# Three accumulators in turn in layers 2 and 3, and the end of a layer-3 tile in four pieces

## The chip, the cores and the metric

The kernel runs on one core of a Trainium2 chip. The metric is the device time of one execution in microseconds (us). The times shown are medians of several executions, beside one execution that the hardware profiler recorded.

The engines are named as in the profile: PE (TensorE, with PEld for its weight loads), DVE (VectorE), ACT (ScalarE), POOL (GpSimd, which here issues the indirect loads), and SP (SyncE, which here issues the direct loads and stores). The engines run side by side, and each takes its own instructions in their order.

## The reference, cut to what matters

Four graph layers on 4096 nodes with 256 features; `adj` is sparse in its later rows and denser in the first. The change touches layers 2 and 3:

```
def layer2(x, adj, H_v):
    scores = x @ H_v                                  # one score a node
    logits = where(adj != 0, adj * scores[None, :], lowest)
    weights = softmax(logits, over the neighbours)
    return weights @ x

def layer3(x, adj, weight, bias):
    neighbours = adj @ x                              # 4096 x 256
    edges = einsum('ij,ji->i', adj, adj)[:, None]     # known since layer 0
    support = concatenate((x, neighbours, edges), axis=1)
    return support @ weight + bias                    # 513 x 256

x = layernorm(x + layer2(x, adj, H_v))
x = layernorm(x + layer3(x, adj, weight, bias))
```

Layers 0 and 1 (a plain adjacency product, and two steps of attention that keeps only the largest weights) come before and stay as they are.

## The kernel before

The nodes are cut into 32 tiles of 128. In layers 2 and 3 the work of a tile is a sum over neighbour columns, taken up in one PSUM accumulator on PE, and then an end that reads the accumulator.

There are two kinds of tiles. The first tiles are hubs: six in layer 2, three in layer 3 (`HUBS`, line 41). A hub goes over all 32 column tiles, in 8 chunks of 4: a panel of the transposed adjacency is loaded by SP, four buffers in turn, and each chunk gives 4 matmuls (`all_columns`, lines 1049 to 1057, in layer 2; `adj_matmul`, lines 166 to 180, in layer 3). All other tiles are listed: of each, `CAPS[I]` gathered columns of 4 to 16 entries a row are used. The packed weights (`pc`) are loaded by SP in blocks of at most 5 columns, and for each column POOL gathers 128 rows of features with an indirect DMA (`xg`, line 353) into one of 16 buffers. `listed_steps` (lines 396 to 410) then makes one matmul a column and yields after each. `listed_matmul` runs it to its end.

The order of tiles is that of `mixed(n)`: the listed tiles from the last to the first, with a hub after each run of them. In layer 2 the runs have 4 tiles, in layer 3 they have 8.

In layer 2 the weights of a column are made first: ACT takes the exp (line 1029), DVE multiplies by the mask (line 1030), into one of four `pe` buffers. The end of a tile is on DVE: `rk`, from the last column of the accumulator (lines 1072 and 1073), `y` = accumulator times `rk` plus the tile's own features (line 1061), and the layernorm. `y` is the last reader of the accumulator. The result goes to a DRAM array `x3d`, and stays in the core's memory as `X3`.

In layer 3 the end of a tile is `out_3` (lines 1077 to 1090): `nb`, a copy of the accumulator on ACT, which is its last reader; four transposes on PE into one PSUM tile, two of the tile's own features and two of `nb`; `xT`, a copy of them on ACT; four output matmuls into `po`; a bias term `t` on DVE; the sum, the layernorm, and the store by SP.

Both layers take the accumulators "R" and "A" in turn, so that tile n writes where tile n-2 has been read out. A third PSUM area, two banks under the tag "lg", serves the logits of layer 1 and lies unused in layers 2 and 3.

Apart from the attention loops of layer 1, the order in which instructions stand on their engines is not written by hand: a planner runs through the program with a model of its own, and puts on each engine, among the instructions that it holds ready, the one that comes first in program order. So the place of a line in the program is a priority, and waits on the chip can differ from those that the planner saw.

Of the kernel before, what the change touches and what calls it, by code (L numbers as in the profile page):

```python
# [11 lines left out]
F32 = mybir.dt.float32  # L12
# [6 lines left out]
P = 128  # L19
N = 4096  # L20
D = 256
# [35 lines left out]
LC = 512  # L57
# [5 lines left out]
def gnn_kernel(ctx: ExitStack, tc: tile.TileContext, x, pair, W0, W1T, W2T, W3T, U1T, U2T,  # L63
# [99 lines left out]
    adjT_v = pair.rearrange("(t p) b s i -> p t b s i", p=P)  # L163
    pair_r = pair.rearrange("j b s i -> (j b) (s i)")

    def adj_matmul(ps, rhs, I, seen=None, width=D, beside=None):

        for c in range(NT // JC):
            a = pools["loads"].tile([P, JC, P], F32, name="panel", tag="panel")
            nc.sync.dma_start(a, adjT_v[:, c * JC:(c + 1) * JC, I, 1])  # L170
            if seen is not None:
                nc.vector.tensor_reduce(seen[:, c * JC:(c + 1) * JC, I], a, AX.X, OP.max, apply_absolute_value=True)
            if beside is not None:
                beside(c)
            if callable(rhs):
                b = rhs(c)
            for k in range(JC):
                j = c * JC + k
                r = b[:, k, :] if callable(rhs) else rhs[j][:, :width]
                nc.tensor.matmul(ps[:, :width], a[:, k, :], r, start=(j == 0), stop=(j == NT - 1))  # L180

    def acc_tile(which):
        return psum.tile([P, 512], F32, name="acc", tag=f"acc{which}")
# [24 lines left out]
    def transposed(tiles, name):  # L208

        n = 2 * len(tiles)  # L210
        pt = psum.tile([P, 4, P], F32, name="ptx", tag="ms", bufs=2)
        for s, t in enumerate(tiles):
            for h in range(2):
                nc.tensor.transpose(pt[:, 2 * s + h, :], t[:, h * P:(h + 1) * P], ident)
        xT = work.tile([P, 4, P], F32, name=name, tag="xT")
        nc.scalar.copy(xT[:, :n, :], pt[:, :n, :])  # L216
        return xT
# [53 lines left out]
    def run(gen):  # L271
        for _ in gen:
            pass
# [111 lines left out]
    def unpack(I):  # L385
        parts = []
        for m, (a, b) in enumerate(pieces(I)):
            if step_one[0]:
                pc = pools["gat"].tile([P, PIECE, 2, P], F32, name="pc2", bufs=n_blocks[0])[:, :, 1]
            else:  # L390
                pc = pools["gat"].tile([P, PIECE, P], F32, name="pc", bufs=4)
            nc.sync.dma_start(pc[:, :b - a], packed[I][m])
            parts.append(pc)
        return parts

    def listed_steps(ps, src, width, I, parts, use=None, stop=True):

        n = 0
        for pc, (a, b) in zip(parts, pieces(I)):
            xs = []  # L400
            for k in range(a, b):
                xg = pools["gat"].tile([P, src.shape[1]], F32, name="xg", padded_shape=[P, D + 2])
                gather(xg, src, idx_x, col(I, k))
                xs.append(xg)
            if use is not None:
                pc = use(pc, xs, b - a)
            for k in range(b - a):
                nc.tensor.matmul(ps[:, :width], pc[:, k, :], xs[k][:, :width], start=(n == 0), stop=stop and n == CAPS[I] - 1)  # L408
                n += 1
                yield  # L410

    def listed_matmul(*args, **kw):
        run(listed_steps(*args, **kw))
# [402 lines left out]
    def times_u(pz, xT, u, start, stop):  # L816
        for h in range(2):
            nc.tensor.matmul(pz, xT[:, h, :], u[:, h, :], start=start and h == 0, stop=stop and h == 1)  # L818

    def pz_tile():  # L820
        return psum.tile([P, D], F32, name="pz", tag="ms", bufs=2)
# [218 lines left out]
    def mixed(n):  # L1040

        listed = list(range(NT - 1, n - 1, -1))
        step = -(-len(listed) // (n + 1))
        order = []
        for k in range(n + 1):
            order += listed[k * step:(k + 1) * step] + [k] * (k < n)
        return order

    def all_columns(ps, I):
        for c in range(NT // JC):  # L1050
            a = pools["loads"].tile([P, JC, P], F32, name="panel", tag="panel")
            nc.sync.dma_start(a, adjT_v[:, c * JC:(c + 1) * JC, I, 1])
            xs = X2[c * JC:(c + 1) * JC]
            e = nbr_weights(a, xs, JC)
            for k in range(JC):
                j = c * JC + k
                nc.tensor.matmul(ps[:, :D + 1], e[:, k, :], xs[k][:, :D + 1], start=(j == 0), stop=(j == NT - 1))
# [5 lines left out]
        nc.sync.dma_start(x3d[rows(I), :], x3)  # L1063

    for n, I in enumerate(mixed(HUBS[0])):
        ps = acc_tile("A" if n % 2 else "R")
        if I < HUBS[0]:
            all_columns(ps, I)
        else:
            listed_matmul(ps, x2d, D + 1, I, unpack(I), nbr_weights)  # L1070
        rk = one("rk", bufs=3)
        nc.vector.tensor_scalar_max(rk, ps[:, D:D + 1], 1e-37)
        nc.vector.reciprocal(rk, rk)
        out_2(I, ps, rk, X2[I][:, :D], X3[I])


    def out_3(I, ps, x3):
        nb = work.tile([P, D], F32, name="nb")
        nc.scalar.copy(nb, ps[:, :D])
        t = work.tile([P, D], F32, name="y")  # L1080
        nc.vector.scalar_tensor_tensor(t, web, edge[:, I:I + 1], b3b, op0=OP.mult, op1=OP.add)
        nc.vector.tensor_add(t, t, x3)
        xT = transposed([x3, nb], "xT3")
        po = pz_tile()
        for a in range(2):
            times_u(po, xT[:, 2 * a:2 * a + 2], wl[a], a == 0, a == 1)
        nc.vector.tensor_add(t, t, po)
        o = pools["late"].tile([P, D], F32, name="o", padded_shape=[P, D + 2])
        layernorm(o, t)
        nc.sync.dma_start(out[rows(I), :], o)  # L1090

    for n, I in enumerate(mixed(HUBS[1])):
        ps = acc_tile("A" if n % 2 else "R")
        if I < HUBS[1]:
            adj_matmul(ps, X3, I)
        else:
            listed_matmul(ps, x3d, D, I, unpack(I))
        out_3(I, ps, X3[I])


    def rows4(src, more=0):
# [35 lines left out]
    def with_all_columns():  # L1137
        for I in range(LE, NT):
            ps = acc_tile("A")
            adj_matmul(ps, rows4(x, 1), I, width=D + 1)  # L1140
            xin = reload(x, I)
            for _ in out_0(I, ps, ps[:, D:D + 1], xin, xin):
                pass
        feats = [pools["e"].tile([P, D], F32, name=f"all_{I}", bufs=1) for I in range(NT)]
        for I in range(NT):
            nc.sync.dma_start(feats[I], xd[0][rows(I), :])
        for n in range(2):
            U[n] = [load_u(n, s) for s in range(2)]
            if n:
                for I in range(NT):  # L1150
                    nc.sync.dma_start(feats[I], xad[rows(I), :])
            for I in range(NT):
                old = reload(xd[n], I)
                psr = acc_tile("R")
                adj_matmul(psr, rows4(xd[n]), I)
                xf = new_xf(I, psr, old)
                e, rk = attn_any(n, I)
                psa = acc_tile("A")
                weighted_sum(psa, e, feats)
                if n:  # L1160
                    run(out_1(I, xf, new_xa(xa_tile(1, I), psa, rk)))
                else:
                    xa = new_xa(work.tile([P, D], F32, name="xa3", tag="z"), psa, rk)
                    nc.sync.dma_start(xad[rows(I), :], xa)
                    run(out_a0(I, xa, feats))
                    run(out_f0(I, xf))
        sb = pools["e"].tile([P, N], F32, name="score_b", bufs=1)
        for g in range(NT // 4):
            pt = psum.tile([P, 4, P], F32, name="pt", tag="tp", bufs=2)
            for k in range(4):  # L1170
                j = g * 4 + k
                nc.tensor.transpose(pt[:, k, :], scores[:, j:j + 1].to_broadcast([P, P]), ident)
            nc.scalar.copy(sb[:, g * 512:(g + 1) * 512], pt.rearrange("p a b -> p (a b)"))
        for I in range(NT):
            nc.sync.dma_start(feats[I], x2d[rows(I), :D])
        for I in range(NT):
            e, rk = nbr_any(I, sb)
            ps = acc_tile("A" if I % 2 else "R")
            weighted_sum(ps, e, feats)
            out_2(I, ps, rk, feats[I], work.tile([P, D], F32, name="x3", tag="z"))  # L1180
        for I in range(NT):
            x3 = reload(x3d, I)
            ps = acc_tile("A" if I % 2 else "R")
            adj_matmul(ps, rows4(x3d), I)
            out_3(I, ps, x3)

    leave()
    enter(e=1, loads=2, tmp=1)
# [32 lines left out]
```

## Time and profile before

| | us |
|---|---|
| median of 3 runs | 3561.51 (3556.79 to 3567.95) |
| the profiled execution | 3550.94 |
| its span, first to last instruction | 3549.1 |
| layer 2, about | 3018 to 3258 of the span |
| layer 3, about | 3258 to 3540 of the span |

Over the whole span PE is busy for 2701.3 us (76%), DVE for 2392.3 (67%), ACT for 1507.7 (42%) and POOL for 1087.6 (31%). The granted clock of PE is 0.879 of full speed in the mean.

How to read the lines below. A line of a timeline gives the start in us, the duration in us, the engine, the line of the program, the operation, what it writes and reads, the shape and the number of instructions merged; in brackets stands the engine's idle time before it and who ended it. "issue" there is idle time in which the profile shows no wait, and "remote" a semaphore that moved without an instruction that ended just before. A matmul in fp32 has two records and two weight loads. A line of the view of waits gives the waiting engine, tile and line, then whom it waited for: us in total, times, longest.

### The profile page before, as it was taken

The page shows a single profiled execution, that of the slowest core. Times are in us where ns is not written, and L with a number is a line of the kernel's source. Part 1 is how long each engine was busy: PE and PEld are TensorE (multiplying, and loading weights), DVE is VectorE, ACT ScalarE, POOL GpSimd, SP SyncE. Part 2 cuts the span into 40 slices and gives each one's busy share as a digit, 9 for nine tenths or more (in the row PEclk, how much of TensorE's full clock was granted, in tenths as well). Part 3 has the DMA queues.
Part 4 walks back from the last instruction along what each step waited for, and adds up shares of the span by engine and source line. Part 5 has one row for each costly group of instructions (what it writes and reads, how often), then busy time and mean ns, then how long its engine had stood idle before and what let it go on. Part 6 is the DMA issues. An engine that isn't in the chain of part 4 may idle for free.

```text
span 3549.1 us, 41701 instructions
## 1 busy us (share of the span) xinstructions
PE 2701.3 (76%) x12372; PEld 2028.7 (57%) x12372; DVE 2392.3 (67%) x8384; ACT 1507.7 (42%) x2655; POOL 1087.6 (31%) x1266
## 2 busy tenths in 40 slices
PE   6776778979999999954766666666666676666776
PEld 4554555757777777833555555555555455555565
DVE  5774449946666766439788888888888884554444
ACT  0000013323333433367666666666666661443110
POOL 1025340056544333230322221112111113553553
PEclk9997879989999999976888888888888898787898
DMA  9965430033332222140111111111111114554443
GB/s 281 278 188 151 134 114 22 9 104 110 102 100 85 81 64 67 58 128 2 58 46 47 41 41 36 33 40 38 36 35 35 36 34 124 173 175 140 142 151 97
DMA packets 346509, 322.86 MB, mean 91 GB/s; under 512 B 32032, under 2 KB 305840, under 8 KB 346272
## 3 DMA queue, kind: packets, MB, share of 16 engines
q1 hardware_dynamic: 281696, 187.30, 18.2%
q0 software_dynamic: 43328, 118.63, 11.1%
q10 hardware_dynamic: 21248, 14.16, 1.3%
q8 instruction: 101, 1.65, 0.2%
q14 instruction: 136, 1.11, 0.1%
HBM read 272.48 MB, written 47.48 MB: 90 GB/s over the span
## 4 chain that ended last, share of the span: by engine, by line
PE 53%; DVE 19%; ACT 11%; issue 6%; DMA 5%; another core or an unknown queue 4%; POOL 2%; ACTq 0%; POOLq 0%; DVEq 0%; SPq 0%
PE acc L204 18%; PE lg L513 8%; PE acc L408 7%; DVE cand L685 5%; PE pz L818 5%; PE acc L180 5%; PE pt L193 5%; DVE tmp L683 4%; DMA half<-in_pair 4%; ACT junk L618 4%; ACT junk L619 3%; DVE top L696 2%; ACT junk L584 2%; DVE rest L698 2%
## 5 line engine op out<-in xcount | busy, mean ns | idle before, releaser
L353 POOL DMA_INDIRECT xg<-xd,idx_x x360 | 470.4, 1307 | 1031.9 <-PE acc L408 905.3
L513 PE MATMUL lg<-kT,qi 64*128 64x512 f32 x1024 | 335.4, 720 | 406.6 <-ACT junk L584 395.9
L195 ACT COPY eT<-pt 128x512 f32<-128x512 f32 x512 | 295.5, 584 | 581.1 <-PE pt L193 540.2
L204 PE MATMUL acc<-xa,eT 128*128 128x256 f32 x2048 | 506.5, 394 | 42.6 <-ACT eT L195 42.6
L204 PE MATMUL acc<-x,eT 128*128 128x256 f32 x2048 | 495.6, 386 | 0.3 <-ACT eT L195 0.3
L204 PEld LDWEIGHTS acc<-xa,eT 128*128 128x128 f32 x2048 | 404.4, 200 | 123.7 <-ACT eT L195 56.0
L204 PEld LDWEIGHTS acc<-x,eT 128*128 128x128 f32 x2048 | 387.8, 193 | 81.3 <-issue 20.0
L408 PE MATMUL acc<-xg,pc 128*128 128x256 f32 x1156 | 386.9, 435 | 26.6 <-DMA xg<-x3d,idx_x 11.1
L513 PEld LDWEIGHTS lg<-kT,qi 64*128 64x128 f32 x1024 | 87.4, 204 | 462.5 <-ACT junk L584 407.9
L581 ACT ACTIVATE e<-lg 128x1024 f32<-128x1024 f32 x256 | 262.2, 1024 | 182.6 <-PE lg L513 156.7
L193 PE MATMUL pt<-ident,e 128*128 128x128 f32 x2048 | 301.7, 275 | 31.1 <-DVE h L599 13.0
L408 PEld LDWEIGHTS acc<-xg,pc 128*128 128x128 f32 x1156 | 208.1, 208 | 203.5 <-issue 148.2
L180 PE MATMUL acc<-xw,panel 128*128 128x257 f32 x1024 | 269.1, 413 | 65.2 <-DMA panel<-in_pair 40.9
L193 PEld LDWEIGHTS pt<-ident,e 128*128 128x128 f32 x2048 | 252.5, 142 | 77.4 <-issue 32.0
L618 ACT ACTIVATE junk<-e,hm 128x2048 bf16<-128x2048 f32 x128 | 256.0, 2000 | 77.7 <-DVE hm L613 67.6
L180 PEld LDWEIGHTS acc<-xw,panel 128*128 128x128 f32 x1024 | 199.4, 204 | 118.9 <-DMA panel<-in_pair 50.2
L619 ACT ACTIVATE junk<-e,h 128x2048 bf16<-128x2048 f32 x128 | 256.4, 2003 | 2.9
L676 DVE MAX8 cand<-e 128x8 f32<-128x128 f32 x1024 | 214.7, 278 | 49.6 <-ACT e L581 48.2
L685 DVE MAX8 cand<-tmp 128x8 f32<-128x128 f32 x1024 | 204.2, 277 | 2.2
L216 ACT COPY xT<-ptx 128x256 f32<-128x256 f32 (+1 forms) x160 | 74.0, 463 | 305.5 <-DMA panel<-in_pair 113.0
L353 POOL DMA_INDIRECT pc<-in_pair,idx_a x180 | 174.7, 970 | 83.0 <-issue 47.2
L703 POOL COPY f_x<-ex 128x1 f32<-128x1 f32 x64 | 11.6, 181 | 601.2 <-DVE ex L702 601.2
(243 smaller groups left out, 4393.9 us busy)
## 6 DMA issues: line engine op xcount, KB each, us to landing
panel<-in_pair SPq DMA_DIRECT2D x200, 256.0 KB
half<-in_pair SPq DMA_DIRECT2D x64, 512.0 KB
pc<-pk SPq DMA_DIRECT2D x55, 320.0 KB
z<-z SPq DMA_DIRECT2D x128, 128.0 KB
pc<-pk SPq DMA_DIRECT2D x45, 256.0 KB
xin<-xd SPq DMA_DIRECT2D x64, 128.0 KB
xg<-xd,idx_x POOLq DMA_INDIRECT x360
pc<-pk SPq DMA_DIRECT2D x23, 192.0 KB
```

What stands on the lines that cost most here:

```text
L180: nc.tensor.matmul(ps[:, :width], a[:, k, :], r, start=(j == 0), stop=(j == NT - 1))
L193: nc.tensor.transpose(pt[:, k, :], e[:, (g * 4 + k) * P:][:, :P], ident)
L195: nc.scalar.copy(eT[g], pt)
L204: nc.tensor.matmul(ps[:, :D], eT[g][:, k, :], rhs[j][:, :D], start=(j == 0), stop=(j == NT - 1))
L353: nc.gpsimd.indirect_dma_start(out=o, out_offset=None, in_=src, in_offset=bass.IndirectOffsetOnAxis(ap=idx[:, c], axis=0))
L408: nc.tensor.matmul(ps[:, :width], pc[:, k, :], xs[k][:, :width], start=(n == 0), stop=stop and n == CAPS[I] - 1)
L513: nc.tensor.matmul(ps[:, h, :], qi[r, :], kT[r, (n * NC + c) * LC:][:, :LC], start=True, stop=True)
L581: nc.scalar.activation(both(e, c), ps, AF.Exp, accum_out=s8[:, c:c + 1])
L618: nc.scalar.activation(junk, ec, AF.Relu, bias=hm, accum_out=part[:, c:c + 1])
L619: nc.scalar.activation(junk, ec, AF.Sign, bias=a["h"], scale=-1.0, accum_out=below[:, c:c + 1])
L676: nc.vector.max(cand[:, g, :], e[:, g * SEG:(g + 1) * SEG])
L685: nc.vector.max(cand[:, c * (NS // 2) + g, :], w[:, g * SEG:(g + 1) * SEG])
```

## The change

Three things are changed. `acc_of(n)` hands out "R", "A" and the first bank of "lg" in turn, for both layers. `out_3` becomes a generator of four pieces: the copy of `nb`; the transposes and the copy of `xT`; the output matmuls of the tile's own features and the term `t`; the output matmuls of `nb`, the sum, the layernorm and the store. And the loop of layer 3 runs the first piece behind a tile's own matmuls, and each of the others behind a chunk of the next tile: after every column of a listed tile, after every four columns of a hub. What is left is run when the next tile's matmuls are all issued. The reserve path for dense inputs, `with_all_columns`, which isn't taken here, runs the four pieces at once.

```diff
-    def adj_matmul(ps, rhs, I, seen=None, width=D, beside=None):
+    def adj_matmul(ps, rhs, I, seen=None, width=D, beside=None, behind=None):
...
                 nc.tensor.matmul(ps[:, :width], a[:, k, :], r, start=(j == 0), stop=(j == NT - 1))
+            if behind is not None:
+                behind()
...
+    def acc_of(n):
+
+        return psum.tile([P, 2, LC], F32, name="lg", tag="lg")[:, 0, :] if n % 3 == 2 else acc_tile("RA"[n % 3])
...
     for n, I in enumerate(mixed(HUBS[0])):
-        ps = acc_tile("A" if n % 2 else "R")
+        ps = acc_of(n)
...
     def out_3(I, ps, x3):
         nb = work.tile([P, D], F32, name="nb")
         nc.scalar.copy(nb, ps[:, :D])
+        yield
+        xT = transposed([x3, nb], "xT3")
+        yield
+        po = pz_tile()
+        times_u(po, xT, wl[0], True, False)
         t = work.tile([P, D], F32, name="y")
         nc.vector.scalar_tensor_tensor(t, web, edge[:, I:I + 1], b3b, op0=OP.mult, op1=OP.add)
         nc.vector.tensor_add(t, t, x3)
-        xT = transposed([x3, nb], "xT3")
-        po = pz_tile()
-        for a in range(2):
-            times_u(po, xT[:, 2 * a:2 * a + 2], wl[a], a == 0, a == 1)
+        yield
+        times_u(po, xT[:, 2:4], wl[1], False, True)
         nc.vector.tensor_add(t, t, po)
         o = pools["late"].tile([P, D], F32, name="o", padded_shape=[P, D + 2])
         layernorm(o, t)
         nc.sync.dma_start(out[rows(I), :], o)

+    end = iter(())
     for n, I in enumerate(mixed(HUBS[1])):
-        ps = acc_tile("A" if n % 2 else "R")
+        ps = acc_of(n)
         if I < HUBS[1]:
-            adj_matmul(ps, X3, I)
+            adj_matmul(ps, X3, I, behind=lambda: next(end, None))
         else:
-            listed_matmul(ps, x3d, D, I, unpack(I))
-        out_3(I, ps, X3[I])
+            for _ in listed_steps(ps, x3d, D, I, unpack(I)):
+                next(end, None)
+        run(end)
+        end = out_3(I, ps, X3[I])
+        next(end)
+    run(end)
...
-            out_3(I, ps, x3)
+            run(out_3(I, ps, x3))
```

`times_u(pz, xT, u, start, stop)` makes the two matmuls of one half of `xT` against one half of the output weights; `transposed` makes the transposes and the copy; `run` steps a generator to its end.

## The prediction

> **What bounds the kernel now.** The profiled execution took 3550.94 us around a span of 3549.1; the median of the three runs is 3561.51. I make the sum against the profiled execution and carry the difference over to the median. A measurement of this kernel tells 0.3% (10.7 us) from no change.
>
> I read the page first, then busy time by stretch for layers 2 and 3, then who waited for whom, then timelines around the waits. From the page, the span and the chain of work that ended last, in which PE has the most:
>
> ```profile
> span 3549.1 us, 41701 instructions
> PE 53%; DVE 19%; ACT 11%; issue 6%; DMA 5%; another core or an unknown queue 4%; POOL 2%; ACTq 0%; POOLq 0%; DVEq 0%; SPq 0%
> ```
>
> Only the last 522 us are touched. In the view of busy time by stretch (time, then busy us and instructions of PE, PEld, DVE, ACT, POOL; granted clock, DMA share, GB/s) layer 2 is the first line and layer 3 the second:
>
> ```profile
> 3018.00:3258.00 240.00, 166.43 (x630) 135.52 (x630) 131.67 (x528) 98.42 (x310) 115.22 (x116) 0.81 0.57 168
> 3258.00:3540.00 282.00, 210.63 (x872) 163.88 (x872) 125.56 (x452) 30.63 (x64) 139.65 (x146) 0.88 0.43 132
> ```
>
> No engine is full. Back to back, a 256-column matmul here takes 0.43 us (two records, 0.215 each), so layer 2's 315 matmuls need 136 us of 240. Layer 3 has 242 adjacency matmuls (104 us), 128 output matmuls (55) and 128 transposes of 0.11 (14): 173 of 282. A gather starts 1.25 us after the one before: 126 x 1.25 = 158 us in layer 2, 146 x 1.25 = 183 in layer 3. What is left over is waiting on PE: idle stretches of over 0.7 us from start to start add up to 76 us in layer 2 and 72 in layer 3. The waits of layer 2 (total, times, longest) show that the gathers are not the limit: they stand still for want of free buffers.
>
> ```profile
> POOL xg L353 <- PE acc L408: 84.0, 17, 17.3
> ...
> DVE rk L1072 <- remote: 36.6, 6, 9.2
> ```
>
> "remote" is no other core here. It is a signal of PE that comes long after the modelled end of the matmul that sends it. I took all idle stretches of PE over 1.2 us in the whole trace: in 86 of them the last matmul's signal came at its modelled end, with 0.12 gathers per us being issued meanwhile; in 45 it came late, by 0.3 to 9.7 us, with 0.64 gathers per us. So late signals go with POOL issuing gathers; the change leaves all 272 gathers of layers 2 and 3.
>
> An ordinary tile of layer 3 in the timeline:
>
> ```profile
> 3423.99 0.60 PE L408 MATMUL acc<-xg,pc 128*128 128x256 f32 x2
> 3424.03 0.37 ACT L1079 COPY nb<-acc 128x256 f32<-128x256 f32 x1 [3.44 <-PE acc L408]
> 3424.46 0.44 PE L214 MATMUL ptx<-ident,nb 128*128 128x128 f32 x2
> ...
> 3424.73 1.03 PE L408 MATMUL acc<-xg,pc 128*128 128x256 f32 x4
> ...
> 3424.99 0.58 ACT L216 COPY xT<-ptx 128x512 f32<-128x512 f32 x1 [0.58 <-issue]
> ...
> 3425.62 1.99 PE L818 MATMUL pz<-wl,xT 128*128 128x256 f32 x8
> ```
>
> The reader should see that the planner already weaves the end of a tile into the next one: one matmul of the next tile covers the copy of nb, two cover the copy of xT, and PE has no gap. It goes wrong where a signal is late, also in front of a hub:
>
> ```profile
> 3326.54 0.37 ACT L1079 COPY nb<-acc 128x256 f32<-128x256 f32 x1 [4.21 <-remote]
> ...
> 3326.97 0.44 PE L214 MATMUL ptx<-ident,nb 128*128 128x128 f32 x2 [1.51 <-issue]
> ...
> 3330.14 3.43 PE L818 MATMUL pz<-wl,xT 128*128 128x256 f32 x8 [1.87 <-ACT xT L216]
> ```
>
> The hub's 32 matmuls need nothing of this end, but 29 of them stand behind it. In layer 2 the start of a hub is the place (PE, then DVE):
>
> ```profile
> 3102.95 2.40 PE L408 MATMUL acc<-xg,pe 128*128 128x257 f32 x10 [2.75 <-ACT pe L1029]
> 3113.25 4.20 PE L1057 MATMUL acc<-x,pe 128*128 128x257 f32 x9 [7.89 <-DVE y L1061]
> ```
>
> ```profile
> 3099.65 0.69 DVE L1030 SCALAR_TENSOR_TENSOR pe<-panel,pe 128x512 f32<-128x512 f32 x1 [1.51 <-issue]
> ...
> 3102.23 0.47 DVE L1061 SCALAR_TENSOR_TENSOR y<-acc,rk,x 128x256 f32<-128x256 f32 x1
> ...
> 3110.93 0.16 DVE L1072 TENSOR_SCALAR rk<-acc 128x1 f32<-128x1 f32 x1 [7.65 <-remote]
> ...
> 3111.51 0.69 DVE L1030 SCALAR_TENSOR_TENSOR pe<-panel,pe 128x512 f32<-128x512 f32 x1
> ...
> 3112.63 0.47 DVE L1061 SCALAR_TENSOR_TENSOR y<-acc,rk,x 128x256 f32<-128x256 f32 x1
> ```
>
> The hub's first chunk is ready at 3100.34, PE is free at 3105.35, yet its first matmul waits until 3113.25: its accumulator is still held by the tile two places before, whose y is read out at 3112.63. The tile three places before was read out at 3102.70.
>
> [...]
>
> **The change part by part.**
>
> *Third accumulator, layer 2.* No instruction is added; tile n now waits for y of tile n-3. With listed tiles L1 to L4 ahead of a hub, the hub waits for y of L2 in place of L3. What comes last then is the mask of a later chunk, which stands on DVE behind rk of L3. Hub by hub:
> - Hub 0: PE idles 1.46 us after two x3 transposes of layer 3 that the planner put there, and 5.72 us before them. If they stay there: 1.5; if not, up to 7.
> - Hub 1: last listed matmul over at 3072.59, first hub matmul 3077.89, and three chunks were masked by 3071.44: 5.3.
> - Hub 2: chunk 0 runs at once; chunk 1 is masked at 3112.20, so matmul 5 starts near 3112.3 in place of 3116.81 (before, the first four ran at half clock): 4.5. Bound 7.9.
> - Hub 3: likewise, PE free at 3143.45, chunk 0 masked 3136.37, chunk 1 at 3149.30; matmul 5 started at 3153.91: 4.5. Bound 6.9.
> - Hub 4: started without a wait: 0.
> - Hub 5: 8.1 us idle, two chunks masked by 3224.69, but the third waits behind an rk at 3234.57, whose signal is 13 us late. If that signal keeps its time, nothing; if it follows PE's restart, 8. I take 2.
> Sum 17.8; bounds 5 (hub 1 alone) and 35 (7 + 5.3 + 7.9 + 6.9 + 8). The gathers can follow: a group of four tiles and a hub has at most 21, so 26 us of issue, in a period of 34 to 42 us.
>
> *Third accumulator, layer 3.* Tile n+2's first matmul already comes after n's nb copy in PE's order: 0.
>
> *End of a listed layer-3 tile in pieces.* The same 4 transposes, 4 output matmuls, 2 copies and DVE work. In program order the next tile's first matmul now precedes the transposes and its second the first output half. By readiness the planner should give nearly today's order, with the two x3 transposes (0.22 us) and that matmul swapped: xT was not ready after one covering matmul before, or the output matmuls would have gone there. 29 tiles: 0; bounds -10 (late signals hit less) and +13.6 (rows above: nb's transpose at 3424.46 to xT over at 3425.57 and matmul at 3425.62 is 1.16 us; with one covering matmul 0.27 + 0.43 = 0.70 are filled, 0.46 open, times 29).
>
> *The end ahead of a hub, layer 3.* Four hub matmuls (1.73 us), then the transposes, four more, half the output. The waits in today's three hubs: 1.51 + 1.87, 0.42, 3.17 = 7.0 us; output matmuls at half clock, 3.43 against 1.99: 1.4. Gone, 8.4; at least 3, since a wait can come up at the hub's own end.
>
> *Queues.* SP: out of tile n now comes after the next tile's pc loads in program order. No PE wait in layer 3 is put down to pc or panel, so 0. POOL: gathers keep their order. ACT: nb stays where it was. DVE: the t operations (0.48 + 0.42) move behind the transposes; DVE is busy 126 of 282 us, so 0. The last tile has no next one: 0.
>
> Sum: -17.8 - 8.4 = -26, so 3525 beside 3550.94, and 3561.5 - 26 = 3535.5 beside the median. I take 3536.
>
> **The rivals.**
> - *Late signals keep the total (no change).* They are as many as before, and a wait that is lifted at a hub's start comes back at chunk 1 or 2. For it: rk and y stand in order on DVE, and layer 3's listed tiles keep their order. Against it: hub 1 had three chunks ready. A quarter of the sum: 3555.
> - *Late signals hit much less (larger gain).* With PE running on, the pieces absorb some of the 60 us of waits in layer 3's listed tiles too, and layer 2 gives its bound: -35 - 8 - 10 = -53, so 3508. Against it: covering matmuls per piece stay one or two.
> - *The hub moves ahead of the listed tile (slower).* With its accumulator free, the planner can put hub chunks before L4's matmuls, which it may expect late. With one chunk that is a gain; from two on, L4 stands on PE behind chunk 1's mask (3112.20 in hub 2, against its start at 3102.95). Then its 2.2 us no longer fill the wait, and its gather buffers are freed some 12.7 us later, against 9 us of POOL's spare time: 2.2 + 3.7 = 5.9 a hub, four hubs, +23.6; less 8.4 in layer 3, +15: 3577. Against it: chunk 1's own exps are behind L4's in most groups.
>
> **How the numbers follow.** Forecast 0.43, no change 0.25, larger gain 0.13, slower 0.19. The forecast's own range is 3520 to 3550. For 8 in 10 the range takes in most of the larger gain and the near part of the slower case: 3512 to 3575. Faster 0.56, within 0.3% 0.25, slower 0.19.
>
> **What would show it.** Right: in the timeline of layer 2, first hub matmuls right behind the last listed one, with releaser mask (L1030) instead of y; in layer 3, four hub matmuls before the nb transposes and no PE idle there; listed tiles still one matmul, transposes, two matmuls, output. Wrong: output halves split by a matmul with a wait before them in every listed tile; hub chunks ahead of listed matmuls with POOL's wait for PE grown over 84 us; or layer 2's idle time unchanged with the wait on DVE's mask.

## The result and the profile after

The changed kernel took 3575.55 us (median of 4 runs, 3567.25 to 3576.99) beside 3559.15 us for the kernel before (4 runs, 3555.87 to 3567.95): ratio 1.0037, 95% interval 1.0013 to 1.0062. It was forecast at 3536 us, within 3512 to 3575: in place of a gain of 0.7% there is a small loss, and the time lies half a microsecond beyond the range. That half microsecond is chance: two later measurements beside a kernel before of this speed, below, have 3553.36 and 3564.84 us. The three together put the loss nearer to 0.13%, hardly clear of nothing, and none shows the forecast gain.

The profiled execution took 3576.76 us. From its page, the span and the chain of work that ended last:

```profile
span 3575.0 us, 41686 instructions
...
PE 51%; DVE 20%; ACT 11%; DMA 6%; another core or an unknown queue 6%; issue 5%; POOL 1%; ACTq 0%; SPq 0%; POOLq 0%; DVEq 0%
```

PE's share of the chain went from 53 to 51%, and the share that the profile can't give to a releaser on this core rose from 4 to 6%. Line numbers are now two to six higher in the lines shown here. The first gather of layer 2 starts at 3016.7 us, where it was at 3005.2: of the 26 us between the two spans, 11.5 lie ahead of layer 2, where nothing was changed. They are chance: two later profiles of the changed kernel have 3004.6 and 3016.5 us there. Busy time by stretch (time, then busy us and instructions of PE, PEld, DVE, ACT, POOL; granted clock, DMA share, GB/s), cut at the same places of the work as before, layer 2 and then layer 3:

```profile
3029.60:3275.40 245.80, 166.14 (x630) 135.07 (x630) 130.58 (x528) 97.95 (x310) 115.10 (x116) 0.83 0.56 164
3275.40:3565.90 290.50, 212.03 (x872) 168.81 (x872) 126.85 (x452) 30.63 (x64) 139.29 (x146) 0.84 0.43 129
```

Counts and busy times of every engine are those of before, and both stretches are longer: 245.8 beside 240, 290.5 beside 282. The added time is waiting. Who waited for whom in layer 2 of the changed kernel:

```profile
ACT pe L1031 <- remote: 52.1, 7, 12.2
...
DVE rk L1078 <- remote: 41.3, 6, 8.5
POOL xg L355 <- PE acc L410: 36.3, 9, 12.8
...
POOL xg L355 <- PE lg L410: 26.0, 3, 13.3
...
PE lg L1063 <- DVE pe L1032: 16.4, 2, 9.0
...
PE acc L1063 <- DVE pe L1032: 12.1, 2, 6.3
```

and in layer 2 of the kernel before:

```profile
POOL xg L353 <- PE acc L408: 56.2, 14, 15.2
...
ACT pe L1029 <- remote: 43.4, 6, 11.6
...
PE acc L1057 <- DVE y L1061: 7.9, 1, 7.9
...
PE acc L408 <- DVE y L1061: 6.1, 2, 5.1
...
PE acc L1057 <- DVE pe L1030: 2.1, 2, 1.9
```

PE's waits changed in kind. Its 14.0 us for y are gone, and those for the mask `pe` went from 2.1 to 28.5 us. The late signals of PE ("remote") cost ACT's exponentials more than before, 52.1 beside 43.4 us, and 54.3 to 65.8 in three later profiles with the third accumulator. For rk, 41.3 beside 36.6 us tells nothing, since these later profiles have 18.0 to 54.1. The last fence also shows a slip of the prediction. It gave POOL's wait in layer 2 as 84.0 us; that answer was for a stretch that began at 2955 us, still in layer 1. Layer 2 itself has 56.2, and after the change 36.3 + 26.0 = 62.3.

The place to look at is the start of a hub. This is the timeline of the changed kernel at the third one (start, us, engine, line, what; in brackets the idle time before it):

```profile
3115.84 4.09 PE L410 MATMUL acc<-xg,pe 128*128 128x257 f32 x10 [2.40 <-issue]
...
3119.74 1.93 PE L1063 MATMUL lg<-x,pe 128*128 128x257 f32 x8
...
3121.91 0.71 DVE L1032 SCALAR_TENSOR_TENSOR pe<-panel,pe 128x512 f32<-128x512 f32 x1
...
3122.67 2.00 PE L1063 MATMUL lg<-x,pe 128*128 128x257 f32 x8 [1.00 <-issue]
...
3126.88 0.95 POOL L355 DMA_INDIRECT xg<-x2d,idx_x  x1 [0.30 <-issue]
3130.07 0.94 POOL L355 DMA_INDIRECT xg<-x2d,idx_x  x1 [2.25 <-remote]
...
3132.05 0.16 DVE L1078 TENSOR_SCALAR rk<-acc 128x1 f32<-128x1 f32 x1 [8.47 <-remote]
3132.05 1.28 ACT L1031 ACTIVATE pe<-panel,x 128x128 f32<-128x128 f32 x4 [9.45 <-remote]
...
3132.92 0.69 DVE L1032 SCALAR_TENSOR_TENSOR pe<-panel,pe 128x512 f32<-128x512 f32 x1
...
3133.67 0.80 PE L1063 MATMUL lg<-x,pe 128*128 128x257 f32 x1 [9.00 <-DVE pe L1032]
```

The third accumulator did what it was to do: the hub's first four matmuls (eight records) start right behind the last listed one, with no wait for y. Four more follow at 3122.67. Then PE stands for 9 us. The mask of chunk 2 stands on DVE behind rk of the last listed tile, and rk waits for the signal of a matmul whose modelled end is 3115.84 + 4.09 = 3119.93. It comes 12 us later: POOL stopped issuing gathers at 3127.83, the first signals came through 2.2 us later (they release POOL itself at 3130.07), and rk followed at 3132.05. ACT, whose next exponentials also wait for PE, starts in the same 10 ns as rk. The wait that was lifted at chunk 0 is back at chunk 2. A matmul's end is modelled, but PE went on with the hub's matmuls at 3119.74 and 3122.67, which speaks for a late signal and against PE itself being held.

Layer 3's order at a hub is the forecast one, and in this profile PE does not stand there:

```profile
3348.42 1.89 PE L180 MATMUL lg<-x,panel 128*128 128x256 f32 x8
3350.14 0.38 PE L216 MATMUL ptx<-ident,x 128*128 128x128 f32 x2
3350.36 0.38 PE L216 MATMUL ptx<-ident,nb 128*128 128x128 f32 x2
3350.58 1.89 PE L180 MATMUL lg<-x,panel 128*128 128x256 f32 x8
3352.31 1.03 PE L820 MATMUL pz<-wl,xT 128*128 128x256 f32 x4
```

Yet the layer's start is worse. Its second tile waits for xT, whose copy waits for PE, while POOL issues one gather after the other every 1.25 us and stops at 3308.59:

```profile
3307.64 0.95 POOL L355 DMA_INDIRECT xg<-x3d,idx_x  x1 [0.30 <-issue]
3312.66 0.58 ACT L218 COPY xT<-ptx 128x512 f32<-128x512 f32 x1 [21.84 <-remote]
3312.93 0.94 POOL L355 DMA_INDIRECT xg<-x3d,idx_x  x1 [4.35 <-remote]
...
3313.29 3.78 PE L820 MATMUL pz<-wl,xT 128*128 128x256 f32 x8 [19.05 <-ACT xT L218]
```

PE stands for 19 us where the kernel before stood for 11.3 in the same place. In later profiles on such a chip a kernel that leaves layer 3 as it was has 16 us here, and three with the change's layer 3 have 13 to 20, so how much of the difference is the change's can't be said. The stand itself is there in all of them.

### The profile page after: what moved, and what is told of

Its sections match the earlier page's. It is cut to its first block, busy times and chain, and to the rows that moved or that the text cites. A ratio compares the mean times of both kernels' runs of the same rounds, so it can differ in the third digit from the quotient of the medians.

```text
span 3575.0 us, 41686 instructions
## 1 busy us (share of the span) xinstructions
PE 2706.6 (76%) x12372; PEld 2037.5 (57%) x12372; DVE 2392.4 (67%) x8384; ACT 1507.4 (42%) x2655; POOL 1087.7 (30%) x1266
## 4 chain that ended last, share of the span: by engine, by line
PE 51%; DVE 20%; ACT 11%; DMA 6%; another core or an unknown queue 6%; issue 5%; POOL 1%; ACTq 0%; SPq 0%; POOLq 0%; DVEq 0%
PE acc L206 17%; PE lg L515 8%; PE acc L410 7%; DVE cand L687 6%; PE pz L820 4%; PE pt L195 4%; DVE tmp L685 4%; DMA half<-in_pair 4%; ACT junk L620 4%; ACT junk L621 3%; PE acc L180 3%; DVE top L698 2%; DVE rest L700 2%; PE acc L1063 2%
## 5 line engine op out<-in xcount | busy, mean ns | idle before, releaser
L410 PE MATMUL acc<-xg,pc 128*128 128x256 f32 x1088 | 368.9, 441 | 26.8 <-DMA xg<-x3d,idx_x 11.4
L410 PEld LDWEIGHTS acc<-xg,pc 128*128 128x128 f32 x1088 | 199.0, 210 | 203.5 <-issue 153.7
```

## The experiments

**Theory.** PE's signals are often late while POOL issues gathers back to back (in the kernel before, 45 of 131 idle stretches of PE begin with a late one, with 0.64 gathers per us beside 0.12 in the others). A hand-over from PE to DVE or ACT and back then costs a delay that mostly ends soon after POOL has stopped (2.2 us after it at the third hub above). The change alters which hand-over meets the delay, not how many gathers there are. **Rivals.** The loss comes from the new order of layer 3; or the forecast gain of layer 2 is there and layer 3 loses it; or it is chance.

The runs fell on two kinds of chip, which the kernel before tells apart: it takes 3542 to 3580 us on one and 3321 to 3340 on the other. The measurement above and the profile of the prediction are of the first. I call them the late and the prompt chip, for a reason that the first experiment shows; whether it is the chip or something around it is not known. Every ratio is taken on one chip.

**1. Both kernels again, unchanged.**

> The kernel before, unchanged, for a second profile, to see how much the single stretches differ from one execution to the next. If the lengthening by 5.9 us (layer 2) and 8.5 us (layer 3) between the two profiles is the change's, layer 2 (first gather of its own to the first of layer 3) takes 254.8 us again to within 2, and layer 3 to the end 289 to within 3. If it is chance of one profile, they spread by 5 us or more.

> The changed kernel, unchanged, for a second profile. If its loss is the change's: layer 2 some 260 us, layer 3 some 297, and again four hub matmuls at once and then 5 to 9 us of idle PE at every hub of layer 2, and a wait of some 19 us at the second tile of layer 3. If it is chance, the 19 us wait is gone and layer 3 is near 289.

The prompt chip ran them: 3329.13 and 3318.83 us, one run each. Neither expectation had thought of that, and it was the most useful result of all. Layers 2 and 3 of the kernel before on this chip, by stretch:

```profile
2938.00:3115.00 177.00, 148.56 (x630) 123.61 (x630) 130.40 (x528) 100.46 (x310) 118.82 (x116) 0.94 0.75 228
3115.00:3318.00 203.00, 188.61 (x872) 148.94 (x872) 125.63 (x452) 30.63 (x64) 139.60 (x146) 0.96 0.59 184
```

These are the stretches that the prediction read as 240 and 282 us, with the same instructions and the same busy POOL. I repeated the count of idle stretches of PE over 1.2 us, whole trace: of those with a signal that can be read, 45 of 131 began with a late one on the late chip, and none of over 100 on the prompt chip. Of the 63 and 79 us that the two stretches lose on the late chip, 47 and 63 are PE standing (idle stretches over 0.7 us add up to 76 and 72 us there, 29 and 9 here); the granted clock of 0.81 and 0.88 beside 0.94 and 0.96 goes with it.

**2. The change and its halves, each kind of chip.** The third accumulator in layer 2 alone, layer 3 as before:

```diff
     for n, I in enumerate(mixed(HUBS[0])):
-        ps = acc_tile("A" if n % 2 else "R")
+        ps = acc_of(n)
```

> The third accumulator in layer 2 alone; layer 3 as before. Theory (PE's signals come late while the gathers are issued, so the wait lifted at a hub's start comes back at its second chunk): layer 2 between 254 and 262 us, with four hub matmuls at once and 5 to 9 us behind them, the whole 0 to +7 us. Rival (the prediction's sum was right in layer 2 and layer 3's pieces lose it): layer 2 235 to 245 us, the whole -10 to -18.

> The third accumulator in layer 2 alone, once more. Theory: beside a kernel before of some 3555 us, ratio 0.9985 to 1.002, layer 2 253 to 262 us, a wait of 5 to 9 us behind the first four hub matmuls of most hubs. Rival (the prediction's sum for layer 2, -17.8 us): 0.994 to 0.997 and layer 2 at 237 to 245 us. Beside 3330 us: 0.9985 again.

> The third accumulator in layer 2 alone. Theory: beside a kernel before of some 3555 us, ratio 0.998 to 1.002, with a wait of 5 to 12 us behind the first four or eight hub matmuls of most hubs in place of the one before them. Rival (the prediction's sum for layer 2, -17.8 us): 0.994 to 0.997, layer 2 at 237 to 245 us. Beside 3330 us: 0.999 again.

The pieces of layer 3 alone (the end of a tile split up as in the change), two accumulators everywhere:

```diff
+    end = iter(())
     for n, I in enumerate(mixed(HUBS[1])):
         ps = acc_tile("A" if n % 2 else "R")
...
-            adj_matmul(ps, X3, I)
+            adj_matmul(ps, X3, I, behind=lambda: next(end, None))
...
-            listed_matmul(ps, x3d, D, I, unpack(I))
-        out_3(I, ps, X3[I])
+            for _ in listed_steps(ps, x3d, D, I, unpack(I)):
+                next(end, None)
+        run(end)
+        end = out_3(I, ps, X3[I])
+        next(end)
+    run(end)
```

> The end of a layer-3 tile in pieces, two accumulators everywhere. Theory (the swap in the listed tiles only moves a wait, the hubs gain their 7 us): layer 3 285 to 292 us, the whole -5 to +4. Rival (the pieces are what loses): layer 3 295 to 300 us, the whole +6 to +12, layer 2 254.8 as before.

> The pieces of layer 3 alone, two accumulators. Theory: beside a kernel before of some 3555 us, ratio 0.998 to 1.002, layer 3 282 to 295 us. Rival (the pieces bring the loss): 1.002 to 1.004, layer 3 at 295 us and more. Beside 3330 us: 0.9993 again.

The whole change again:

> The changed kernel again, timed in five rounds beside the kernel before. Theory (the loss comes only where the signals of PE are late while gathers are issued; where they are on time, as in the second profiles, the change gains a little): beside a kernel before of some 3330 us the ratio is 0.997 to 0.9995 and no idle stretch of PE begins with a late signal; beside one of some 3560 us the ratio is 1.002 to 1.006 and some 40 stretches begin with one. Rival (the change loses by its own order, whatever the signals do): 1.002 to 1.006 in both.

> The changed kernel once more, five rounds, to settle whether its 0.37% of loss is real. Theory (no effect where signals are late, since a lifted wait returns at the next chunk): beside a kernel before of some 3555 us, ratio 0.998 to 1.002; beside one of some 3330 us, 0.996 to 0.9995. Rival (a true loss of 0.3 to 0.4% where signals are late): 1.002 to 1.005 beside 3555.

> The changed kernel once more, to settle whether its loss is real. Theory (nothing gained or lost where signals are late): beside a kernel before of some 3555 us, ratio 0.998 to 1.002. Rival (a true loss of 0.3 to 0.4% there): 1.002 to 1.005. Beside 3330 us: 0.998 again.

| kernel | late chip: ratio to before (95%) | prompt chip: ratio to before (95%) |
|---|---|---|
| whole change | 1.0037 (1.0013 to 1.0062), first measurement; 0.9995 (0.9975 to 1.0015); 1.0013 (0.9998 to 1.0027) | 0.9983 (0.9975 to 0.9991) |
| third accumulator in layer 2 | 1.0014 (1.0002 to 1.0026) | 0.9985 (0.9976 to 0.9995); 0.9991 (0.9983 to 0.9999) |
| pieces in layer 3 | 0.9996 (0.9981 to 1.0011) | 0.9993 (0.9985 to 1.0002) |

On the late chip the three intervals of the whole change have only 1.0013 to 1.0015 in common: a loss of some 5 us, within what one measurement can't tell from nothing. The first measurement seems to show it too large, and the 1.002 to 1.006 that I had expected of the repeat was missed (0.9995). The third accumulator alone gives much the same, 1.0014. The pieces alone can't be told from nothing. So the rival that put the loss into layer 3 finds no support, and the one that saw the forecast gain in layer 2 falls. The third accumulator in layer 3 was not run alone. On the prompt chip the change gains 0.17%, 5.7 us.

From the traces, in us: layer 2 from its first gather to layer 3's first, layer 3 from there to the end, and PE's idle stretches over 0.7 us in each.

```
                               layer 2  layer 3   idle 2  idle 3
late:   before                  254.8    289.1      76      72
        pieces alone            251.8    291.8      77      73
        accumulator alone       258.7    289.9      82      71
        whole, first            260.7    297.6      83      76
        whole, second           257.4    283.7      78      66
        whole, third            258.4    293.3      81      70
prompt: before                  192.0    210.3      29       9
        accumulator alone       185.9    210.9      28       9
        whole, timed            188.8    212.5      24       8
```

The four profiles with the third accumulator here have 257.4 to 260.7 us in layer 2, the two without have 251.8 and 254.8. Layer 3 has no such order. The timeline of PE in the kernel with the accumulator alone, on the late chip, shows why:

```profile
3136.41 4.06 PE L408 MATMUL acc<-xg,pe 128*128 128x257 f32 x10 [2.20 <-PE lg L408]
3140.31 1.90 PE L1057 MATMUL acc<-x,pe 128*128 128x257 f32 x8
3144.83 2.00 PE L1057 MATMUL acc<-x,pe 128*128 128x257 f32 x8 [2.63 <-issue]
3154.42 5.94 PE L1057 MATMUL acc<-x,pe 128*128 128x257 f32 x13 [7.59 <-DVE pe L1030]
```

The hub now meets the delay twice, 2.6 and 7.6 us, where the kernel before met it once (6.9 us at this hub) and then ran its 32 matmuls in one go. The next table has all six hubs of layer 2 together, in every profile with 16 buffers on the late chip. It gives PE's idle time over 0.7 us in front of a hub's first matmul, between its 32, and elsewhere in layer 2. It is counted as in the brackets, from the end of the matmul before, so the sums are some 8 us lower than in the table above.

```
                               in front  inside  elsewhere
before                           29.7      7.1      31.9
pieces alone                     28.5      9.5      29.8
accumulator alone                 3.5     53.4      16.4
whole, first                      1.7     55.9      17.5
whole, second                     1.6     50.7      17.8
whole, third                      1.7     54.3      17.0
```

So the third accumulator did lift waits, in front of the hubs even more than the forecast 17.8 us and some 14 us in the listed tiles as well. Inside the hubs 41 to 49 us came back. On the prompt chip a hub of the whole change is nearly without a gap:

```profile
2972.43 3.71 PE L1063 MATMUL acc<-x,pe 128*128 128x257 f32 x16 [1.03 <-ACT pe L1031]
2976.29 10.67 PE L1063 MATMUL acc<-x,pe 128*128 128x257 f32 x48 [0.15 <-DVE pe L1032]
```

**3. No gathers in layers 2 and 3.** Both kernels with the gathers there replaced by plain loads of 128 rows in a row, the same bytes, issued by SP (they leave out the gather by list, so other rows are added up); and the kernel before with the same loads issued by POOL:

```diff
-                gather(xg, src, idx_x, col(I, k))
+                if src is x2d or src is x3d:
+                    J = (I + k) % NT
+                    nc.sync.dma_start(xg[:, :src.shape[1]], src[J * P:(J + 1) * P, :])
+                else:
+                    gather(xg, src, idx_x, col(I, k))
```

> The kernel before with the gathers of layers 2 and 3 replaced by plain loads of 128 rows in a row, issued by SP; it leaves out the gather by list, so other rows are added up, with as many bytes. Theory (late signals go with POOL issuing gathers): beside a kernel before of some 3560 us, no late signal in layers 2 and 3, and they take 190 to 205 and 205 to 225 us in place of 255 and 289; beside one of some 3330 us, where no signal is late, they change by less than 15 us together. Rival (signals are late from the load of the DMA engines or from the clock): they stay at 250 and 285 beside 3560.

> The changed kernel with the gathers of layers 2 and 3 replaced by plain loads that SP issues, as in the run of the kernel before with such loads (146 us from the first load of layer 2 to the last, 213 us for layer 3); it leaves out the gather by list. Theory (without late signals the change gains what its own waits were worth): layer 2 140 to 147 us, layer 3 203 to 212 us. Rival (the changed order loses by itself): 150 us and more, 215 us and more.

> The kernel before with the gathers of layers 2 and 3 replaced by plain loads of 128 rows in a row that POOL issues; it leaves out the gather by list, so other rows are added up. Theory (late signals go with POOL's indirect gathers): beside a kernel before of some 3555 us, no more than 5 late signals in layers 2 and 3, which take 150 to 200 and 205 to 225 us. Rival (any DMA that POOL issues does it): late signals as with the gathers, layers at 230 us and more. Beside 3330 us none is late in either, and the two layers take 145 to 195 and 205 to 215 us.

All three fell on the late chip. They took 3373.38, 3369.54 and 3390.03 us (one run each) beside 3552.93 and, for the last two, 3558.86. Layers 2 and 3 of the kernel before with SP's loads, by stretch:

```profile
3010.90:3158.10 147.20, 131.25 (x580) 111.14 (x581) 116.80 (x476) 95.34 (x299) 0.00 (x0) 0.96 0.90 266
3158.10:3362.00 203.90, 194.42 (x932) 157.84 (x930) 138.55 (x505) 36.88 (x84) 0.00 (x0) 0.99 0.65 198
```

and with POOL's loads:

```profile
3016.20:3169.80 153.60, 132.01 (x550) 110.19 (x550) 110.14 (x447) 92.03 (x289) 67.18 (x127) 0.91 0.81 245
3169.80:3388.20 218.40, 201.21 (x960) 163.44 (x960) 145.42 (x536) 39.77 (x95) 77.86 (x146) 0.97 0.63 191
```

No signal is late in layers 2 and 3, in any of the three; ahead of them, where the gathers stayed, some 20 still are in each. With SP's loads PE's idle stretches in the two layers are 14 and 1 us in place of 76 and 72, and the granted clock is 0.96 and 0.99 in place of 0.81 and 0.88. So late signals go with POOL's indirect gathers. They do not go with the clock: in the profile of the kernel before, 37 of the 45 late stretches begin while the clock is granted in full. They do not go with the load of the DMA engines (266 GB/s here, 168 before), and not with POOL issuing DMAs as such. Nor is it the number or the size of the packets: from layer 2's first load on, POOL's queue moves 13056 packets and 35.80 MB both in the kernel before and with POOL's plain loads, in the same sizes. The rivals named in the expectations fall. What in a gather holds the signals, and why on one kind of chip only, stays open. Layer 2 came out shorter than I had written (147 in place of 190 to 205), because POOL's 1.25 us for a gather (126 x 1.25 = 158) no longer set a floor either.

With signals on time like this, the change takes layers 2 and 3 together from 360.4 to 361.7 us, with idle time of 14 and 1 going to 10 and 2. The after-version of this run had been expected at 140 to 147 and 203 to 212 us; it has 150.4 and 211.3, so layer 2 missed its range, and 3 us between single runs show neither gain nor loss. There is no gain of 26 us in the change even where no signal is late: on the prompt chip, in the table above, the third accumulator is worth 3 to 6 us in layer 2.

**4. Fewer and more buffers for gathered rows.** The kernel before with 8 in place of 16, and the changed kernel with 24:

```diff
-    enter(gat=16, x3=1, loads=4)
+    enter(gat=8, x3=1, loads=4)
```

> The kernel before with 8 buffers for gathered rows in layers 2 and 3 in place of 16. Theory (PE's signals are held up for as long as POOL goes on issuing gathers, so PE stands until POOL has filled its buffers): beside a kernel before of some 3555 us, the longest stand behind the first tile of layer 3 falls from 11.7 to 19.4 us to 10 or less, since POOL stops after 8 gathers of 1.25 us, and stretches above 6 us in layers 2 and 3 become fewer; the whole between -15 and +10 us. Rival (signals are late for a time of their own, whatever POOL has in store): the stretches stay as long and the whole loses 5 to 20 us, because the gathers start later. Beside 3330 us, where nothing is late: +2 to +15.

> The changed kernel with 24 buffers for gathered rows in layers 2 and 3 in place of 16. Theory (the gathers' run-ahead is worth time, as 8 buffers showed: +78 us beside 3332; where signals are late, a longer burst of gathers only makes PE stand longer): beside a kernel before of some 3330 us, -6 to -20 us; beside one of some 3555, -10 to +10 us, with a stand of 20 us or more at the second tile of layer 3. Rival (16 are already enough): -6 us beside 3330, as the changed kernel alone.

Eight fell on the prompt chip: 3410.2 beside 3331.69 us, ratio 1.0231 (1.021 to 1.0252), +79 us where I had written +2 to +15. The waits of its layer 2:

```profile
ACT pe L1029 <- DMA xg<-x2d,idx_x: 92.5, 62, 13.0
POOL xg L353 <- PE acc L408: 84.2, 45, 12.8
```

The kernel before has 45.1 and 17.0 us in these two rows on that chip. A likely reason: most layer-2 tiles need four or five gathered blocks before their weights are all made, so eight buffers hold little more than one tile ahead. The question that the run was made for, whether a shorter burst makes a shorter stand where signals are late, stays open. Twenty-four fell on the late chip: 1.0008 (0.9995 to 1.0021), so nothing more is to be had there; its first burst in layer 3 is 35 gathers long, from 3271.2 to 3313.8 us, and PE's two stands there are 15.3 and 11.9 us, less than the 20 that I had expected of one. The first of them ended at 3303.4, ten microseconds before POOL's last gather of the burst: the transposes were over at 3287.5 and their signal came at 3302.7, while POOL went on. So a signal can come through amid a burst, and the theory's "after POOL has stopped" is not a rule.

**5. Gathers further apart.** The kernel before with a 128x1 addition on POOL ahead of every gather of layers 2 and 3:

```diff
+                if src is x2d or src is x3d:
+                    nc.gpsimd.tensor_scalar_add(xg[:, :1], ones, EPS)
                 gather(xg, src, idx_x, col(I, k))
```

> The kernel before with a 128x1 addition on POOL ahead of every gather of layers 2 and 3 (it writes one column of the buffer that the gather then overwrites; nothing else changes), so that gathers come some 1.5 to 1.6 us apart in place of 1.25. Theory A (the gathers outrun what takes them, and signals wait in the backlog): beside a kernel before of some 3555 us, fewer than 10 late signals in layers 2 and 3 in place of 23, longest idle stretch under 6 us, layer 2 215 to 235 us, layer 3 235 to 270 us, the whole -40 to -80. Theory B (any gather in flight holds the signals): as many late ones, POOL's own among them, so gathers come 2 us and more apart, and the whole is +10 to +60. Beside 3330 us, where nothing is late: +15 to +40, POOL being nearer to the limit.

It fell on the prompt chip: 1.0158 (1.0138 to 1.0179), +52 us where I had written +15 to +40. The timeline of POOL shows gathers 1.55 us apart:

```profile
3178.96 0.23 POOL L404 TENSOR_SCALAR xg<-ones 128x1 f32<-128x1 f32 x1
3179.47 1.01 POOL L353 DMA_INDIRECT xg<-x3d,idx_x  x1 [0.27 <-POOL xg L404]
3180.51 0.23 POOL L404 TENSOR_SCALAR xg<-ones 128x1 f32<-128x1 f32 x1
3181.01 1.08 POOL L353 DMA_INDIRECT xg<-x3d,idx_x  x1 [0.27 <-POOL xg L404]
```

Two repeats fell there too (1.0182 and 1.0167). On that chip it shows only that POOL's issue is close to the limit: 0.3 us on each of 272 gathers is 82 us, and 52 of them are paid. Whether spacing frees the signals on the late chip stays open. No version that still gathers was shown to be faster than the kernel before on the late chip.

## Why the prediction was wrong, point by point

- *What bounds the kernel.* Right that PE stands for late signals and that they go with POOL's gathers; experiment 3 turned that from a count into a shown cause. The 84.0 us of POOL's wait were of the wrong stretch. Two small slips bear on nothing: its own figures make +13.3 of the bound +13.6, and y at hub 2 starts at 3112.63 and is over at 3113.10.
- *Third accumulator, layer 2: -17.8 us.* This step failed. It moved each hub's first matmuls to the moment when they could start and took the rest of the hub along, as if the later chunks' masks kept their old times or came earlier. But these masks stand on DVE behind rk, whose signal mostly comes only after POOL's burst (at hub 2 of the kernel before, rk starts at 3110.93 behind 7.65 us of idle DVE and the next mask at 3111.51). Before, five of the six hubs waited once, in front of their first matmul, and by then the late signals had arrived, so that the 32 matmuls ran through. After, a hub starts early and meets the delay mostly at chunk 1 or 2, often at both: 25 to 28 us less in front of the hubs, 41 to 49 us more inside them. Measured for the third accumulator alone: 1.0014 (1.0002 to 1.0026), some +5 us in place of -17.8. The low bound, 5 us for hub 1 alone "since three chunks were masked", fell too: in the changed kernel that hub ran two chunks and then stood for 7.3 us.
- *Third accumulator, layer 3: 0*, and *the listed tiles in pieces: 0.* Nothing in the runs speaks against either, though neither was run alone. The order is as forecast: one matmul, transposes, two matmuls, output.
- *The end ahead of a hub, layer 3: -8.4, at least -3.* This term failed too. The order came as forecast, and the 7.0 us of idle PE inside the three hubs went to 1.7 with the pieces alone and to none, 5.9 and 0.3 with the whole change. But the pieces alone gave 0.9996, and the layer's idle time stayed at 73 us beside 72. The 7 us were not the hub's: they were late signals that met PE at that place, and an equal time is now lost in listed tiles. On the prompt chip the kernel before does not stand at these places at all (9 us of idle stretches in its whole layer 3), so there was nothing to gain there either. The term's other 1.4 us were a group of output matmuls at a lower clock: over their 3.43 us, from 3330.14, the granted clock was 0.56 in the kernel before (0.50 over the first 4.20 us of hub 2's matmuls, from 3113.25). That they would run faster without the waits was my estimate; the granted clock of layer 3 went from 0.88 to 0.84.
- *Queues: 0.* No wait of PE in the changed kernel's layer 3 says otherwise.
- *The rivals.* "Late signals keep the total" had the mechanism to the letter, down to the wait that "comes back at chunk 1 or 2", and got a chance of 0.25. Its size, a quarter of the gain, was still too kind. The slower rival's mechanism did not occur: in the profile after, the hub's first matmuls stand behind the last listed ones, and POOL's wait for PE in layer 2 grew only from 56.2 to 62.3 us (on the longer stretch that gave 84.0, to 90.1). "Layer 2's idle time unchanged with the wait on DVE's mask", named as a sign of being wrong, is what the profile shows.

The prediction had the evidence for the right answer: 45 late stretches, and a change that leaves all 272 gathers. It then priced waits by what their last releaser was, not by what made that releaser late.

## What to carry to other kernels

A stand of PE is worth its length only if nothing behind it waits for the same thing (here 25 to 28 us less in front of the hubs came with 41 to 49 us more inside them); where signals come in bunches, count the hand-overs that meet a bunch, not the idle time ahead of one of them. If signals are late because of what another engine does, here POOL's indirect gathers, look at that work first: on the late chip a third accumulator moved the wait and took nothing off the time (some 1.0013), 24 buffers gave 1.0008, and leaving out 272 gathers, with plain loads in their place, took 169 to 180 us. A gain of this size needs runs on more than one chip: the same change gave 0.9983 on one kind and some 1.0013 on the other.

## What the hardware did that I had not expected

- The same program, layer by layer the same instructions, took some 3330 us on one kind of chip and some 3555 on the other. In the first profile of each, the time from layer 1's stores to the end went from 405 to 546 us, with POOL and DMA work unchanged; the stretch ahead of it, from the first of these stores to the last, has 0.12 gathers per us in place of 0.50 and takes 1228 us on both.
- On the late chip PE's signals come together soon after a burst of gathers ends: behind the eight bursts of layer 2 of the kernel before, the first four signals within 0.26 us came 0.7 to 5.1 us after the last gather, 2.7 in the median. Not all wait for that: with 24 buffers one signal came amid a burst, 15.2 us past the modelled end of its matmul.
- In the trace of the late chip many signals have no record at all: 4502 of DVE's beside 5204 on the prompt chip, and 707 beside 1804 for one of the gathers' own. The missing ones go with the gathers as the late signals do: layers 2 and 3 have records of 570 of DVE's 981 signals in the kernel before, and none is missing there with plain loads on the late chip. Why they are missing, and whether recording has a part in the late signals, no run here shows; this rival is untested.
- PE's granted clock was lower where PE stood longer: 0.81 in layer 2 with late signals (76 us of idle stretches), 0.94 without them on the other chip (29 us), 0.96 with plain loads (14 us).
